# A tanh recurrence on 128 columns: one step as one block of 128 columns, or as two batches of 64 one behind the other

## The chip, the core and the metric

The kernel runs on one core of one Trainium2 chip. The metric is the device time of one execution in microseconds. The core has five engines that run side by side and meet through semaphores: TensorE (PE in the profile, with its weight loads shown apart as PEld), VectorE (DVE), ScalarE (ACT), GpSimd (POOL) and SyncE (SP, which issues most of the transfers here).

## The reference

An input `x` of 2 batches, 1024 positions and 256 features goes through a small recurrent network, and its states go through a mixture of experts whose result is added to `x`. What matters here is the recurrence:

```python
xW = jnp.einsum('ntd,dh->nth', x, Wx) + b
def step(prev_h, xw_t):
    next_h = jnp.tanh(xw_t + prev_h @ Wh)
    return (next_h, next_h)
_, hs = jax.lax.scan(step, h0, jnp.swapaxes(xW, 0, 1))
```

It runs over all 1024 positions of each of the 2 batches, with a state of 256 features. After it come 8 experts, of which each position takes the 2 with the largest logits:

```python
hidden = jax.nn.silu(x_flat @ wge.T) * (x_flat @ wue.T)
acc + we[:, None] * (hidden @ wde.T)
```

and the sum over the experts is added to the input `x`.

## The kernel before

**The recurrence in parallel.** The 1024 positions of a batch are cut into 64 pieces of 16 (`L = 16`), and all 64 pieces of both batches are stepped at once: the state is 256 features by 128 columns, where a column is a batch b and a piece q. A piece doesn't know the state at its start, so every piece starts early and runs over the pieces before it: these are the warm-up steps. Steps `s` from 8 to 47 warm up, and steps 48 to 63 give the states that are kept, in `hall`. A later check compares the states at the borders of the pieces; if one differs by more than a tolerance, a plain sequential version is run in place of the result.

**One step.** The 256 features are two halves of 128 partitions: `k` counts the halves of the old state, `j` those of the new. A step is, in this order:

- the seed, made two steps ahead: VectorE copies the input's share `xw` into two banks of PSUM, `acc[s % 2][0]` and `acc[s % 2][1]` (function `seed`), one bank for each half j, each 128 columns wide as (b, q). The copy is shifted by `sh` pieces, 3 to 0, so that a warm-up step reads the input of the piece before;
- four matmuls that add to these banks, `Wh` block (k, j) times the old state's half k, 128 columns each (line 611). The order of the four blocks alternates: on even steps (j, k) = (0,0), (1,0), (0,1), (1,1), on odd ones (0,0), (0,1), (1,0), (1,1). After two of them `run(s - 0.5)` emits what is planned for that moment;
- two tanhs on ScalarE (line 639), one for each half j, from the bank to the new state. They go through a helper that records line 49, as all VectorE, ScalarE and GpSimd instructions of this part do.

Up to step 27 (`S16 = 28`) state and weights are f16 in the matmuls; from step 28 on they are f32. From step 28 to step 47 the new state is a tile of shape [128, k, b, q] from a pool with three buffers, except at steps 31 and 47, where it is a tile `inj` that has the start state `h0` in one piece; q0 is then the first piece that the tanh writes. From step 48 on the state goes to `hall`.

**What runs beside it.** Other work is put into the recurrence by an order written out by hand: `at(step, ...)` notes it, `run(step)` emits it. For steps 28 to 47 these are the transfers of the first experts' weights (SyncE), the copy of the input to the output (SyncE, at 28), constant thresholds (GpSimd, at 40), and eight times, at steps 29, 31, 33 and 35 and at 37, 39, 41 and 43, a cast of 128x512 on ScalarE with a subtraction on VectorE behind it, which split the first expert's weights into a high and a low part. All instructions of one engine keep the program's order. After step 48 the routing (logits, one-hot tables, gathers) is worked in, and then follow the experts, which take most of the time.

Of the kernel before, what the change touches and what calls it, by code (L numbers as in the profile page):

```python
# [13 lines left out]
AF = mybir.ActivationFunctionType  # L14
# [5 lines left out]
P = 128  # L20
# [13 lines left out]
S16 = 28  # L34
# [18 lines left out]
def rnn_moe(ctx, tc, xT, xrows, h0T, Wx, Wh, b, gw, W, out):  # L53
    nc = tc.nc
    pe = tc.keep_in_program_order
    vec, act, pool = (InOrder(tc, e) for e in (nc.vector, nc.scalar, nc.gpsimd))
# [67 lines left out]
    def pgu_tile():  # L124
        return pgu.tile([P, 512], F32, name="pgu_t", tag="pgu")

    def ptr_tile():
        return ptp.tile([P, 512], F32, name="ptr", tag="ptr")
# [103 lines left out]
    def start_output():  # L232
# [9 lines left out]
    xw = [  # L242
        hidp.tile([P, 512], F32R, name=nm, tag=nm).bitcast(F32).rearrange("p (j i t) -> p j i t", j=2, i=2)
        for nm in ("hh", "hl")
        for _ in range(4)
    ]
    acc = [[pgu_tile()[:, 0:P] for j in range(2)] for a in range(2)]
# [3 lines left out]
    def fl(t):  # L251
        return t.rearrange("p b q -> p (b q)")

    def bq(t):
        return t.rearrange("p (b q) -> p b q", b=2)
# [17 lines left out]
    def x_split(n, k, eng, low=pool):  # L273
        m = order[n]
        hi, lo = (t[:, k, :] for t in xparts[n % 2])
        x = xs[k][:, m * 2 * P : (m + 1) * 2 * P]
        (act.copy if eng is act else eng.tensor_copy)(hi, x)
        low.tensor_tensor(lo, x, hi.bitcast(F32), ALU.subtract)

    def x_product(n, j):  # L280
        m = order[n]
        pt = ptr_tile()[:, 0 : 2 * P]
        ops = [(wxs[a][:, k, j * P : (j + 1) * P], xparts[n % 2][c][:, k, :]) for k in range(2) for a, c in ((0, 0), (1, 0), (0, 1))]
        for i, (l, r) in enumerate(ops):
            pe(nc.tensor.matmul(pt, lhsT=l, rhs=r, start=(i == 0), stop=(i == len(ops) - 1)))  # L285
        return pt

    def x_store(n, j, pt):
        vec.tensor_scalar(xw[order[n]][:, j].rearrange("p i t -> p (i t)"), pt, bs[:, j : j + 1], None, ALU.add)

    def seed(s, fresh=None):

        sh = 3 - s // L
        r = s % L
        for j in range(2):
            to = bq(acc[s % 2][j])[:, :, sh:64]
            if j == 1 and fresh is not None:
                vec.tensor_scalar(to, bq(fresh[:, r % 2 * P : (r % 2 + 1) * P])[:, :, 0 : 64 - sh], bs[:, j : j + 1], None, ALU.add)
            else:
                copy = act.copy if j == 1 and s >= 50 else vec.tensor_copy  # L300
                copy(to, bq(xw[r // 2][:, j, r % 2, :])[:, :, 0 : 64 - sh])
# [226 lines left out]
    def run(step):  # L528
        for t in sorted(t for t in todo if t <= step):
            for f in todo.pop(t):  # L530
                f()
# [53 lines left out]
    for s, q in ((15, 2), (31, 1), (47, 0)):  # L585
        t = rp.tile([P, 2, 2, 64], F16 if s + 1 < S16 else F32, name=f"inj{s}")
# [12 lines left out]
    vec.tensor_copy(wh16, wh)  # L599
    x_first(1)  # L600
    seed(S0 + 1)
    x_store(1, 0, x_product(1, 0))
    prev = None
    for s in range(S0, 64):
        if s > S0:
            blocks = [(0, 0), (1, 0), (0, 1), (1, 1)] if s % 2 == 0 else [(0, 0), (0, 1), (1, 0), (1, 1)]
            w = wh16 if s < S16 else wh
            for i, (j, k) in enumerate(blocks):
                if i == 2:
                    run(s - 0.5)  # L610
                pe(nc.tensor.matmul(acc[s % 2][j], lhsT=w[:, k, j * P : (j + 1) * P], rhs=prev[k], start=False, stop=True, skip_group_check=True))  # L611
        n, late = (s - S0 + 3) // 2, None
        if n < R // 2:
            pt = x_product(n, (s - S0 + 3) % 2)
            if s % 2 == 0:
                late = n, 1, pt
            else:
                x_store(n, 0, pt)
        elif s < S16:
            pt = ptr_tile()[:, 0:P]  # L620
            for _ in range(2):
                pe(nc.tensor.matmul(pt, lhsT=zl, rhs=zl, start=True, stop=True))  # L622
        q0 = 0
        if s in inj:
            t, q = inj[s]
            q0 = q + 1
            dst = [t[:, k] for k in range(2)]
        elif s >= 48:
            dst = [bq(hall[k][:, s - 48, :]) for k in range(2)]
        else:  # L630
            half = s + 1 < S16
            t = hp.tile([P, 2, 2, 64], F16 if half else F32, name="h16" if half else "h32")
            dst = [t[:, k] for k in range(2)]
        if s == S0:
            q0 = 3 - s // L
            pool.memset(t[:, :, :, 0:q0], 0.0)
        for j in range(2):
            x = bq(xw[s // 2][:, j, s % 2, :])[:, :, 0 : 64 - q0] if s == S0 else bq(acc[s % 2][j])[:, :, q0:64]
            act.activation(dst[j][:, :, q0:64], x, AF.Tanh)
        prev = [fl(d) for d in dst]  # L640
        if s + 2 < 64:
            seed(s + 2, late and late[2])
        if late:
            x_store(*late)
        if s == S0:
            for k in range(2):
                x_split(2, k, act)
        n = (s - S0 + 6) // 2
        if n < R // 2:
            x_split(n, (s - S0) % 2, act)  # L650
        run(s)
# [50 lines left out]
    with ExitStack() as c2:  # L702
# [207 lines left out]
        for n in range(len(steps)):  # L910
            i, s = steps[n]
            u = units[i]
            j = jobs.index(u.job)
# [25 lines left out]
            if 2 <= n < len(steps) - 2:  # L939
                v, t = done[n - 2]  # L940
# [4 lines left out]
        s = NIC - 4  # L945
# [175 lines left out]
```

## Time and profile before

| | us |
|---|---|
| Median of 3 runs (392.15 to 394.67) | 392.47 |
| The profiled execution, its own time | 396.46 |
| Its span, first to last instruction | 394.7 |
| TensorE busy in the span | 372.6 |
| TensorE weight loads busy | 349.5 |
| VectorE busy | 232.3 |
| ScalarE busy | 200.1 |
| GpSimd busy | 118.9 |

One execution was profiled, and every duration is from it. Engines overlap, so busy times don't add up to the span. A line of a group reads: source line, engine, operation, output and inputs with shapes, the number of instructions, then busy time and mean nanoseconds of one, then the idle time ahead of them and what ended it. A line of the timeline reads: start, duration, engine, source line, operation, shapes and count of merged instructions, and in brackets the idle time ahead of it with the engine that ended it. An f32 matmul of the source shows as two instructions on PE and two weight loads on PEld.

### The profile page before, as it was taken

The page shows a single profiled execution, that of the slowest core. Times are in us where ns is not written, and L with a number is a line of the kernel's source. Part 1 is how long each engine was busy: PE and PEld are TensorE (multiplying, and loading weights), DVE is VectorE, ACT ScalarE, POOL GpSimd, SP SyncE. Part 2 cuts the span into 40 slices and gives each one's busy share as a digit, 9 for nine tenths or more (in the row PEclk, how much of TensorE's full clock was granted, in tenths as well). Part 3 has the DMA queues.
Part 4 walks back from the last instruction along what each step waited for, and adds up shares of the span by engine and source line. Part 5 has one row for each costly group of instructions (what it writes and reads, how often), then busy time and mean ns, then how long its engine had stood idle before and what let it go on. Part 6 is the DMA issues. An engine that isn't in the chain of part 4 may idle for free.

```text
span 394.7 us, 7319 instructions
## 1 busy us (share of the span) xinstructions
PE 372.6 (94%) x2715; PEld 349.5 (89%) x2715; DVE 232.3 (59%) x619; ACT 200.1 (51%) x461; POOL 118.9 (30%) x124
## 2 busy tenths in 40 slices
PE   8999999989999999998999999999999999999980
PEld 7998798779997789998999999999989999999970
DVE  6867648897675665565636644465545656644220
ACT  4656676543654543656445553564455555435230
POOL 4770001204272401773042612432040024007032
PEclk9999999999999999999999999999999999999996
DMA  7962323542373433585234444345323306004013
GB/s 222 425 252 76 110 99 104 139 112 56 125 200 108 95 117 125 117 233 143 52 95 48 149 120 134 39 134 135 109 27 111 106 7 151 2 0 48 4 19 39
DMA packets 19291, 43.31 MB, mean 110 GB/s; under 512 B 4832, under 2 KB 14208, under 8 KB 16096
## 3 DMA queue, kind: packets, MB, share of 16 engines
q1 hardware_dynamic: 12432, 32.86, 24.9%
q0 software_dynamic: 6496, 9.09, 13.1%
q10 hardware_dynamic: 320, 0.80, 0.7%
q8 instruction: 24, 0.39, 0.4%
q14 instruction: 19, 0.16, 0.1%
HBM read 36.23 MB, written 10.22 MB: 118 GB/s over the span
## 4 chain that ended last, share of the span: by engine, by line
PE 76%; DMA 8%; DVE 6%; ACT 3%; issue 3%; POOL 1%; POOLq 0%; DVEq 0%; ACTq 0%
PE pgu_t L712 40%; PE yb L865 21%; PE pgu_t L611 8%; DMA out_dram<-y,si 8%; DVE wd L49 3%; PE ptr L285 3%; PE ptr L192 2%; PE pgu_t L865 1%; PE ptr L622 1%; ACT y L874 1%; ACT h L49 1%; PE ptr L339 1%; DMA xg<-rows_d,gidx 1%; DVE mi L49 1%; DVE pgu_t L49 1%
## 5 line engine op out<-in xcount | busy, mean ns | idle before, releaser
L865 PE MATMUL yb<-wd,hh 128*128 128x256 f32 (+2 forms) x560 | 97.7, 284 | 2.5 <-ACT y L874 2.5
L865 PEld LDWEIGHTS yb<-wd,hh 128*128 128x128 f32 (+2 forms) x560 | 83.0, 185 | 5.4 <-ACT y L874 3.7
L728 ACT CAST hh<-g 128x256 fp32r<-128x256 f32 (+5 forms) x96 | 46.7, 489 | 77.0 <-DVE g L720 70.4
L720 DVE TENSOR_TENSOR g<-g,pgu_t 128x256 f32<-128x256 f32 (+5 forms) x96 | 49.8, 522 | 57.0 <-PE pgu_t L712 40.3
L712 PE MATMUL pgu_t<-xhi,gu_g 128*128 128x256 f32 (+5 forms) x384 | 78.5, 326 | 1.3 <-ACT xhi L49 0.6
L453 POOL DMA_INDIRECT out_dram<-y,si x27 | 45.1, 1672 | 113.4 <-ACT y L874 108.8
L712 PE MATMUL pgu_t<-xhi,gu_u 128*128 128x256 f32 (+5 forms) x384 | 77.8, 324 | 0.0
L719 ACT ACTIVATE g<-pgu_t 128x256 f32<-128x256 f32 (+5 forms) x96 | 44.7, 466 | 55.2 <-PE pgu_t L712 50.8
L712 PEld LDWEIGHTS pgu_t<-xhi,gu_u 128*128 128x128 f32 x384 | 61.3, 188 | 4.3
L712 PEld LDWEIGHTS pgu_t<-xhi,gu_g 128*128 128x128 f32 x384 | 58.6, 189 | 4.3 <-issue 1.3
L729 DVE TENSOR_TENSOR hl<-g,hh 128x480 fp32r<-128x480 f32 (+4 forms) x56 | 33.6, 600 | 32.2 <-ACT hh L728 31.6
L865 PE MATMUL yb<-wd,hl 128*128 128x256 f32 (+1 forms) x184 | 51.8, 282 | 0.0
L446 POOL DMA_INDIRECT xg<-rows_d,gi x27 | 29.2, 1080 | 63.9 <-DVE cm L794 56.9
L712 PE MATMUL pgu_t<-xlo,gu_g 128*128 128x256 f32 (+5 forms) x192 | 47.0, 325 | 0.2 <-issue 0.2
L712 PE MATMUL pgu_t<-xlo,gu_u 128*128 128x256 f32 (+5 forms) x192 | 46.5, 323 | 0.0
L712 PEld LDWEIGHTS pgu_t<-xlo,gu_g 128*128 128x128 f32 x192 | 32.5, 188 | 3.0 <-DVE hh L729 0.6
L712 PEld LDWEIGHTS pgu_t<-xlo,gu_u 128*128 128x128 f32 x192 | 32.5, 188 | 2.2
L865 PEld LDWEIGHTS yb<-wd,hl 128*128 128x128 f32 (+1 forms) x184 | 33.7, 183 | 0.1
L611 PE MATMUL pgu_t<-h,wh 128*128 128x128 f32 (+1 forms) x224 | 28.6, 266 | 1.4
L729 DVE TENSOR_TENSOR hh<-g,hh 128x256 fp32r<-128x256 f32 x40 | 16.8, 424 | 14.2 <-ACT hh L728 11.5
L49 ACT ACTIVATE h<-pgu_t 128x128 f32<-128x128 f32 (+1 forms) x72 | 17.6, 276 | 13.9 <-PE pgu_t L611 8.7
L611 PEld LDWEIGHTS pgu_t<-h,wh 128*128 128x128 f32 x152 | 18.4, 190 | 4.2 <-ACT h L49 3.3
(162 smaller groups left out, 462.4 us busy)
## 6 DMA issues: line engine op xcount, KB each, us to landing
raw<-in_W_dram SPq DMA_DIRECT2D x24, 1024.0 KB, 5.0
gu_u<-in_xT_dram SPq DMA_DIRECT2D x6, 256.0 KB, 7.0
rows_e<-gu_u SPq DMA_DIRECT2D x4, 256.0 KB
rows_d<-rows_e SPq DMA_DIRECT2D x1, 528.0 KB
rows_d<-rows_e ACTq DMA_DIRECT2D x1, 528.0 KB, 4.3
out_dram<-in_xrows_dram SPq DMA_DIRECT2D x1, 512.0 KB
rows_d<-rows SPq DMA_DIRECT2D x2, 256.0 KB
rows_d<-gu_u SPq DMA_DIRECT2D x2, 256.0 KB
```

The source lines that it names most:

```text
L49: return lambda *a, **k: self.tc.keep_in_program_order(f(*a, **k))
L192: pe(nc.tensor.transpose(pt[:, m, j, :], tiles[i][:, k * (P + E) : k * (P + E) + P], ident))
L285: pe(nc.tensor.matmul(pt, lhsT=l, rhs=r, start=(i == 0), stop=(i == len(ops) - 1)))
L446: nc.gpsimd.indirect_dma_start(out=xg, out_offset=None, in_=rows[:, :], in_offset=bass.IndirectOffsetOnAxis(ap=idx, axis=0),)
L453: return nc.gpsimd.indirect_dma_start(out=out[:, :], out_offset=bass.IndirectOffsetOnAxis(ap=idx, axis=0), in_=y, in_offset=None, compute_ ...
L611: pe(nc.tensor.matmul(acc[s % 2][j], lhsT=w[:, k, j * P : (j + 1) * P], rhs=prev[k], start=False, stop=True, skip_group_check=True))
L712: pe(nc.tensor.matmul(pt, lhsT=a[i], rhs=b[j], start=(first and i + j + n == 0), stop=(j == 1 and n == len(lhs_rhs) - 1), skip_group_check ...
L719: nc.scalar.activation(g, pg, AF.Silu)
L720: nc.vector.tensor_tensor(g, g, pu, ALU.mult)
L728: nc.scalar.copy(hh, src)
L729: nc.vector.tensor_tensor(hl, src, hh.bitcast(F32), ALU.subtract)
L865: pe(nc.tensor.matmul(yt[0:w, :], lhsT=h[a][:, i * P : i * P + w], rhs=wd[b][:, ic, :], start=(ic == 0 and first and n == 0), stop=(ic == ...
```

## The change

In steps 28 to 47 the division of a step changes from halves to batches. The two banks now belong to the batches: bank z holds both halves j of batch z, 64 columns each, as (j, q). The seed is one copy for each batch. The matmuls are eight, of 64 columns: for batch 0 the four blocks with k outside and j inside, then `run(s - 0.5)`, then the same four blocks for batch 1. The tanhs are one for each batch, reading both halves from the bank and writing both halves of that batch into the state tile, whose layout stays. Steps before 28 and from 48 on are untouched.

```diff
@@ seed @@
         sh = 3 - s // L
         r = s % L
+        if S16 <= s < 48:
+            for z in range(2):
+                vec.tensor_copy(bq(acc[s % 2][z])[:, :, sh:64], xw[r // 2][:, :, r % 2, z * 64 : z * 64 + 64 - sh])
+            return
         for j in range(2):
             to = bq(acc[s % 2][j])[:, :, sh:64]
@@ the loop over s @@
             w = wh16 if s < S16 else wh
+            if S16 <= s < 48:
+
+                for z in range(2):
+                    if z == 1:
+                        run(s - 0.5)
+                    for k in range(2):
+                        for j in range(2):
+                            pe(nc.tensor.matmul(bq(acc[s % 2][z])[:, j, :], lhsT=w[:, k, j * P : (j + 1) * P], rhs=prev[k][:, z * 64 : z * 64 + 64], start=False, stop=True, skip_group_check=True))
+                blocks = ()
             for i, (j, k) in enumerate(blocks):
                 if i == 2:
                     run(s - 0.5)
...
         for j in range(2):
+            if S16 <= s < 48:
+                act.activation(t[:, :, j, q0:64], bq(acc[s % 2][j])[:, :, q0:64], AF.Tanh)
+                continue
             x = bq(xw[s // 2][:, j, s % 2, :])[:, :, 0 : 64 - q0] if s == S0 else bq(acc[s % 2][j])[:, :, q0:64]
             act.activation(dst[j][:, :, q0:64], x, AF.Tanh)
```

In the tanh's new line the loop's `j` counts batches: `t[:, :, j, q0:64]` is both halves of batch j.

## Prediction

> **What bounds the kernel now.** I read the page first (busy times, then the chain that ended last), then the chain in order of time over the recurrence, then the timeline of single steps, then the groups of TensorE kept apart by shape.
>
> ```profile
> PE 372.6 (94%) x2715; PEld 349.5 (89%) x2715; DVE 232.3 (59%) x619; ACT 200.1 (51%) x461; POOL 118.9 (30%) x124
> PE pgu_t L712 40%; PE yb L865 21%; PE pgu_t L611 8%; DMA out_dram<-y,si 8%; DVE wd L49 3%; PE ptr L285 3%; PE ptr L192 2%; PE pgu_t L865 1%; PE ptr L622 1%; ACT y L874 1%; ACT h L49 1%; PE ptr L339 1%; DMA xg<-rows_d,gidx 1%; DVE mi L49 1%; DVE pgu_t L49 1%
> ```
>
> The reader is to see that TensorE sets the time, and that the recurrence's products (L611) are on the ending chain. The change touches steps 28 to 47 alone. They begin with the first f32 run of L611, at 26.73, and end where step 48, the first to read the state `inj` written by step 47, loads its weights at 50.53:
>
> ```profile
> 26.73 0.97 PEld L611 LDWEIGHTS pgu_t<-h,wh 128*128 128x128 f32 x8
> ...
> 49.45 0.97 PEld L611 LDWEIGHTS pgu_t<-h,wh 128*128 128x128 f32 x8 [0.33 <-ACT h L49]
> 49.45 1.16 PE L611 MATMUL pgu_t<-h,wh 128*128 128x128 f32 x8
> 50.20 0.28 ACT L49 ACTIVATE inj<-pgu_t 128x126 f32<-128x126 f32 x1 [0.58 <-PE pgu_t L611]
> 50.51 0.29 DVE L49 COPY pgu_t<-hh 128x128 f32<-128x128 f32 x1 [0.56 <-ACT inj L49]
> 50.53 0.97 PEld L611 LDWEIGHTS pgu_t<-inj,wh 128*128 128x128 f32 x8
> 50.65 0.28 ACT L49 ACTIVATE inj<-pgu_t 128x126 f32<-128x126 f32 x1 [0.17 <-PE pgu_t L611]
> ```
>
> That is 23.80 us for 20 steps, 1.19 each. The x8 says that one f32 step, written as 4 matmuls, is 8 passes, each with a weight load of its own. Eight loads last 0.97 us and a single one 0.19 (below), so one begins every (0.97 - 0.19) / 7 = 0.111 us; 8 passes cost 0.89. The other 0.30 of a step is latency. The chain shows it:
>
> ```profile
> 47.08 2.03 PE pgu_t L611 x14
> 49.10 0.02 issue
> 49.13 0.28 ACT h L49
> 49.41 0.04 issue
> 49.45 2.03 PE pgu_t L611 x14
> ```
>
> Two steps take 2.38 us, in which TensorE issues 16 passes (1.78) and stands still for a tanh for the rest, 0.6. So the most that the change can win is 20 x 0.30 = 6 us, and only if the passes cost no more in total.
>
> What a pass of half the columns costs is decided by these rows (operation, stationary shape, mean ns):
>
> ```profile
> L611 PEld LDWEIGHTS pgu_t<-h,wh 128*128 128x128 f32 x152 | 18.4, 190 | 4.2 <-ACT h L49 3.3
> L865 PEld LDWEIGHTS yb<-wd,hh 128*96 128x96 f32 x48 | 6.7, 163 | 0.0
> L865 PEld LDWEIGHTS yb<-wd,hh 128*32 128x32 f32 x16 | 1.7, 109 | 0.1
> L425 PEld LDWEIGHTS <-wd 128*128 128x128 f16 x32 | 2.2, 97 | 0.9 <-DVE wd L49 0.3
> ```
>
> From 32 to 96 to 128 stationary columns an f32 load grows from 109 to 163 to 190 ns: 27 ns for each 32 columns, over a fixed 82. The part that can't overlap the next load is thus 4 x 27 = 108 ns at 128 columns, and 97 - 82 = 15 ns for f16. The 111 ns between f32 passes is therefore the price of the load, and about that of streaming 128 columns too; the two lie side by side.
>
> **What the Trainium skill says.** "TensorE: Matmul & The Clock Gate", section "LDWEIGHTS (loading the stationary operand)", gives a load as P / 1.2 ns with P the stationary columns: 107 ns for 128. The trace agrees (108 from the rows above), and nothing in it depends on the moving columns. The section "Weight-path perf modes" of the same page says that the fast weight load is on for inputs other than FP32; the trace agrees (15 ns against 108). The section "Back-to-back issue gap" says that the spacing in a stream of load and matmul pairs is set by both. "PSUM — Partial Sum Buffer", section "Summary: rules for kernel authors", wants reads during a matmul to go to another bank; before and after, each tanh reads a bank that is not being written.
>
> **The change part by part.**
>
> *Matmuls.* A step's 4 matmuls of 128 columns become 8 of 64: (k, j) for batch 0, then the same four blocks for batch 1. The weight block changes with every matmul, so none of the loads falls away: 16 passes and 16 loads a step in place of 8 and 8. Streaming 64 columns takes half of about 107 ns, so the load decides. I bound a pass from below by the load, 108, and from above by the largest spacing that passes with both a full f32 load and a comparable stream show here, 12 in 1.42 us at L712, 118 ns. I take 110: a little over the load, since a run of 8 today keeps to 111 while also streaming twice the columns. Step: 16 x 0.110 = 1.76 us.
>
> *The waits that go.* Within step 47 above, the first bank is complete with pass 4. Its load begins at 49.45 + 3 x 0.111 = 49.78, its matmul one load later at 49.90, and tanh begins at 50.20: 0.30 later, of which half a stream (0.05) falls away at 64 columns, 0.25 left. tanh lasts 0.28 (128 elements as before: both halves j of one batch), and 50.48 to 50.53 is 0.05 until the next load. With a step beginning at 0, batch 0's last matmul begins at 8 x 0.11 = 0.88, its tanh runs from 1.13 to 1.41, and batch 0 could go on at 1.46; TensorE is busy with batch 1 until 1.76. Cover: 0.30 us. For batch 1 it is the same, one half step on. All the 0.30 of latency a step is hidden; late next is TensorE itself.
>
> *ScalarE.* Two tanhs a step, as before. Eight times an f32 cast of 128x512 (0.61) stands between batch 1's tanh (ends 2.29) and the next tanh of batch 0 (ready at 2.89): it ends at 2.90. Delay 0.01 against 0.30 of cover: nothing. If the passes were faster, this cover would shrink (rival 2).
>
> *VectorE.* Two seed copies a step as before (0.29 each), of one batch with both halves in place of one half with both batches, 128x124 or 128x126 elements either way. They wait for that batch's tanh of step s and are needed at step s + 2, over 1.5 us later even behind a 0.69 us subtraction. Nothing.
>
> *SyncE, POOL.* The work planned between the blocks by `run(s - 0.5)` is empty for steps 28 to 47 (all its due times there are whole numbers), and no DMA moves in the order.
>
> *The two ends.* Step 28 starts as now: its k = 1 blocks are 4 passes behind its k = 0 blocks in either order. Step 48 has whole-width operands again and needs both tanhs of step 47, so the latency of batch 1's is exposed once: last matmul at 26.73 + 20 x 1.76 = 61.93, tanh 62.18 to 62.46, next load 62.51. From there on all is as before.
>
> *Sum.* Step 48 begins at 62.51 and not at 50.53: 11.98 us later (35.20 + 0.58 - 23.80). Does the rest give some of it back? In the stretch from 50.5 to 76.0, TensorE is busy 24.26 of 25.50 us, from 120 to 385 it is busy 260.32 of 265.00, and its waits between are for ACT, DVE and gathers that the routing itself starts; all of them move with the recurrence. The weights of the first experts land earlier than needed now and have still more time. I give back nothing. The profiled execution took 396.46 us (span 394.7, the rest around it); it would become 408.4. The median of the runs shown is 392.47, 4 us lower than the profiled one; the same addition gives 404.5, or 3.1% more.
>
> **The rivals.**
>
> 1. *False wait between the batches.* A tanh now writes a strided region (two halves, one batch), interleaved with the other batch's. If the k = 1 blocks of batch 0 were made to wait for batch 1's tanh too, they could start at 0.25 + 0.28 + 0.05 + 0.01 = 0.59 after the step's start and not at 0.44, plus a load of 0.11 to refill: 0.25 a step, 5 us, 409.5. Against it: POOL's write of the probabilities into `rows`, interleaved in the same way with two transfers out of that tile, carries no wait for those transfers in the trace's records. Chance 0.05.
>
> 2. *Passes go by moving columns (the other side).* If a pass of 64 columns took half, about 0.058, a step's 16 passes would be 0.93, and the loop of one batch would decide: 8 x 0.058 + 0.25 + 0.28 + 0.05 = 1.05. The eight casts would then push batch 0's tanh by about 0.3 each, 2.3 us. 20 x 1.05 + 2.3 + 0.5 = 23.8: no change, 392.5; without the casts' delay 390. For it: the f16 passes of L425 (8 in 0.61) come every 55 ns, at the stream's rate. Against it: their loads cost 15 ns and these 108. It decides as soon as a pass is under 1.19 / 16 = 0.074. Chance 0.06, of which half is a gain over 1%.
>
> 3. *Load and stream no longer overlap.* A pass would be 108 + 53 = 161 ns, a step 2.58, in all 28 us more: 420.7. For it, only that 64-column f32 passes are not in this trace; against it, load and stream of 128 columns overlap now (111, not 215). Chance 0.04.
>
> 4. *Part is absorbed later*, if the longer recurrence lets early transfers finish before the gathers: TensorE's waits for gathers are only 0.17 and 0.48, so at most some 1 to 4 us, 401. Chance 0.05.
>
> **How the numbers follow.** The forecast, slower with 110 ns a pass, has 0.80. With 108 ns it gives 34.56 + 0.58 - 23.80 = 11.3, so 403.8; with 118 ns 37.76 + 0.58 - 23.80 = 14.5, so 407.0. Widened by a part of rivals 1 and 4, the range is 402.3 to 408.3. Slower by over 1%, which is about what a measurement of this kernel can tell from no change, holds the forecast, rivals 1 and 3, and all of 4: 0.93 with a little rounding down for the unforeseen; within 1%: 0.04; faster by over 1%: 0.03.
>
> **What would show it.** In the changed profile L611 should have 160 more matmul passes and loads than now, f32 with 64 moving columns, beginning every 0.108 to 0.112 us without a gap through steps 28 to 47; no TensorE wait for ACT there; two ACT rows of 128 elements a step, about 0.9 us apart; step 48 beginning near 62.5; and a stretch after it of the same length as now. Spacing under 0.074 us, or ACT waits on TensorE with short passes, would make the forecast wrong, as would a later stage that is over 3 us shorter.

## The result, and the profile after

The changed kernel takes 406.46 us in the median of 4 runs (405.98 to 407.15), the kernel before 392.6 (the median of 4 runs, one more than in the table above): 1.0342 times as long, with an interval of 1.0313 to 1.0371. That is 13.9 us more. The profiled execution took 405.98 us, with a span of 404.1.

The page's first lines of the changed kernel:

```profile
span 404.1 us, 7658 instructions
PE 385.0 (95%) x2875; PEld 366.5 (91%) x2875; DVE 233.8 (58%) x619; ACT 201.0 (50%) x461; POOL 119.7 (30%) x124
```

TensorE has 160 more matmul passes and 160 more weight loads, as the change asks for; the counts of the other engines in this line have not moved. The page's chain of what ended last stops here at a single transfer and shows nothing of the recurrence, so the timeline has to carry the reading. It shows the first steps of the changed stretch:

```profile
27.38 5.77 PEld L619 LDWEIGHTS pgu_t<-h,wh 128*128 128x128 f32 x51
27.46 5.71 PE L619 MATMUL pgu_t<-h,wh 128*128 128x64 f32 x50
...
28.52 0.28 ACT L49 ACTIVATE h<-pgu_t 128x128 f32<-128x128 f32 x1 [1.03 <-PE pgu_t L619]
...
29.41 0.28 ACT L49 ACTIVATE h<-pgu_t 128x128 f32<-128x128 f32 x1 [0.62 <-PE pgu_t L619]
```

A tanh comes every 0.89 us, which is 8 passes, and it is ScalarE that waits for TensorE (1.03 us before the first tanh, then 0.62, in brackets). TensorE waits for no tanh: the loads of this stretch have no idle time before them. 51 loads in a row last 5.77 us: (5.77 - 0.19) / 50 = 0.1116 us from one to the next. The group of the passes of 64 columns shows this idle time in its last column:

```profile
L619 PEld LDWEIGHTS pgu_t<-h,wh 128*128 128x128 f32 x304 | 34.1, 192 | 0.0
L619 PE MATMUL pgu_t<-h,wh 128*128 128x64 f32 x304 | 34.2, 275 | 0.0
```

Where whole-width steps begin again (line 624, step 48), the one exposed wait is seen:

```profile
63.36 0.28 ACT L49 ACTIVATE inj<-pgu_t 128x126 f32<-128x126 f32 x1 [0.62 <-PE pgu_t L619]
...
63.69 0.63 PEld L624 LDWEIGHTS pgu_t<-inj,wh 128*128 128x128 f32 x5 [0.50 <-ACT inj L49]
```

Steps 28 to 47 thus last from 27.38 to 63.69, 36.31 us in place of 23.80: 12.5 us more. A pass of 64 columns costs what one of 128 cost, 0.112 us against 0.111.

### The profile page after: what moved, and what is told of

Read it like the earlier page. It is cut to its first block, busy times and chain, and to the rows that moved or that the text cites. A ratio compares the mean times of both kernels' runs of the same rounds, so it can differ in the third digit from the quotient of the medians.

```text
span 404.1 us, 7658 instructions
## 1 busy us (share of the span) xinstructions
PE 385.0 (95%) x2875; PEld 366.5 (91%) x2875; DVE 233.8 (58%) x619; ACT 201.0 (50%) x461; POOL 119.7 (30%) x124
## 3 DMA queue, kind: packets, MB, share of 16 engines
HBM read 36.23 MB, written 10.22 MB: 115 GB/s over the span
## 5 line engine op out<-in xcount | busy, mean ns | idle before, releaser
L619 PE MATMUL pgu_t<-h,wh 128*128 128x64 f32 x304 | 34.2, 275 | 0.0
L619 PEld LDWEIGHTS pgu_t<-h,wh 128*128 128x128 f32 x304 | 34.1, 192 | 0.0
L745 DVE TENSOR_TENSOR hh<-g,hh 128x256 fp32r<-128x256 f32 x40 | 16.9, 424 | 12.8 <-ACT hh L744 12.5
```

The lines of the kernel that those rows point to most:

```text
L619: pe(nc.tensor.matmul(bq(acc[s % 2][z])[:, j, :], lhsT=w[:, k, j * P : (j + 1) * P], rhs=prev[k][:, z * 64 : z * 64 + 64], start=False, st ...
L745: nc.vector.tensor_tensor(hl, src, hh.bitcast(F32), ALU.subtract)
```

## Experiments

**A second profile of the kernel before.** The first one had waits in the early experts that the changed kernel did not have, which makes a comparison of two single profiles doubtful.

> The kernel before once more, for a second profile. In the first one the span was 394.7 us and TensorE waited in the stretch from 118 to 131 us, at the start of the second expert, for about 1.1 us (xhi, a semaphore, ACT y), which the changed kernel's profile does not show. Theory (these waits belong to that one execution): a span near 391, with the recurrence's steps 28 to 47 again 23.8 us long, and the 3 us shorter stretch from 97 to 147 us. Rival (the change itself shortened the later stages): the waits are there again.

Its time was 393.37 us, its span 391.5. The first table below is this second profile by stage, the second one the changed kernel. A row begins with the stretch and its length; after the comma come busy us and number of instructions of PE, PEld, DVE, ACT and POOL, then the granted TensorE clock, the DMA share and GB/s. The stretches are steps 28 to 47; from step 48 to the first product of the first expert; from there to two groups of transposes among the experts (the third and the fourth row end there); and the rest, to the last matmul.

```profile
27.47:51.28 23.81, 22.37 (x163) 19.37 (x162) 15.47 (x49) 14.44 (x48) 1.05 (x10) 1.00 0.35 115
51.28:80.25 28.97, 26.33 (x243) 24.66 (x243) 22.07 (x142) 18.81 (x70) 3.85 (x8) 1.00 0.39 109
80.25:114.00 33.75, 32.33 (x290) 31.75 (x291) 27.22 (x95) 17.56 (x38) 14.43 (x14) 1.00 0.39 104
114.00:144.60 30.60, 30.60 (x179) 26.59 (x178) 19.88 (x31) 16.25 (x27) 9.67 (x8) 1.00 0.46 137
144.60:379.20 234.60, 233.60 (x1627) 223.26 (x1625) 127.79 (x231) 117.80 (x224) 67.56 (x46) 1.00 0.35 88
```

```profile
27.38:63.69 36.31, 35.94 (x324) 35.81 (x322) 16.71 (x50) 15.23 (x49) 1.06 (x10) 1.00 0.26 88
63.69:92.74 29.05, 26.21 (x243) 24.66 (x243) 21.77 (x141) 18.48 (x69) 3.85 (x8) 1.00 0.35 94
92.74:127.10 34.36, 32.56 (x291) 31.84 (x292) 27.11 (x95) 17.68 (x38) 14.34 (x14) 1.00 0.39 104
127.10:157.70 30.60, 30.60 (x179) 26.57 (x178) 19.87 (x31) 16.22 (x27) 9.63 (x8) 1.00 0.45 134
157.70:392.30 234.60, 233.60 (x1627) 223.26 (x1625) 127.77 (x231) 117.79 (x224) 67.56 (x46) 1.00 0.34 88
```

The recurrence's stretch grew by 12.50 us. The last two stretches are equally long, the two between differ by 0.1 and 0.6. In the first profile of before the last three stretches were 35.34, 32.50 and 235.50 long, so its waits belonged to that execution, and the change neither gave time to the later stages nor took any that these profiles can tell from such scatter. The other traces of the next sections bear this out. From the first load of step 48 to the start of the last matmul it is 327.9 us in the second profile of before, 328.5 and 328.3 in the changed kernel's two profiles, 328.4 with half of the steps changed and 328.4 with the matmuls cut alone; with f16 steps it is 328.3 without the change and 327.7 with it. Which kernels carry the change can't be read from these lengths.

**The changed kernel once more.**

> The changed kernel once more, beside the others on the same chip: 1.034 times the kernel before. Its profile should show the same 0.112 us between passes of 64 columns.

406.46 us against 392.82: 1.0334, interval 1.0309 to 1.0359. The span was again 404.1, and steps 28 to 47 again last 36.3 us, in which the 320 loads come every 0.112 us.

**Half of the steps.**

```diff
-if S16 <= s < 48:
+if S16 <= s < 38:
```

(at the change's three places)

> The change is made in steps 28 to 37 alone, half of the 20; steps 38 to 47 are as before. Theory (each changed step pays 8 more weight loads of 0.112 us and wins back about 0.30 us of waiting): half of the recurrence's loss, 10 x (1.787 - 1.19) + 0.4 at the border where whole-width steps begin again = 6.4 us, so near 399 us. Rival (the loss is a single cost at the end of the warm-up or in the later stages, whatever the number of steps): as large as with all 20 steps, 13 to 14 us, near 406. If 1.3 us of the 13.9 were such a single cost: 7.7, near 400.3.

399.68 us, 1.0169 times before (1.0144 to 1.0193), 6.86 us more: half the loss for half the steps, so the loss is paid step by step. Its profiled execution was the slowest of the six, 402.7 us; step 28 began there at 29.95, 2 to 3 us later than in the other profiles, so only the length of the stretch is read from it. Steps 28 to 47 are 30.3 us long, 6.5 more than before. Where whole-width steps begin again, now at step 38, the wait of the whole change comes again:

```profile
48.39 0.97 PEld L624 LDWEIGHTS pgu_t<-h,wh 128*128 128x128 f32 x8 [0.50 <-ACT h L49]
```

**Only the cut of the matmuls.** The banks, the blocks' order and the tanhs stay those of before. The edit is shown shortened; it holds for steps 28 to 47 alone.

```diff
-pe(nc.tensor.matmul(acc[s % 2][j], lhsT=..., rhs=prev[k], ...))
+for z in range(2):
+    zz = slice(z * 64, z * 64 + 64)
+    pe(nc.tensor.matmul(acc[s % 2][j][:, zz], lhsT=..., rhs=prev[k][:, zz], ...))
```

> Steps 28 to 47 keep the banks, the order of blocks and the tanhs of before (one for each half j); only each matmul of 128 columns is cut into two of 64. So the loads are paid and no batch runs ahead of the other. Theory (loads cost 0.112 each, the batches' independence wins the waits back): 16 passes a step are 1.79 us; tanh of the first half is complete 4 passes before an even step's end, so every second step still waits about 0.2 to 0.3: 20 x 1.787 + 10 x 0.25 = 38.2 for the 20 steps against 23.8 before, 14.5 us more than before, near 407, and about 2 us slower than the changed kernel. Rival (the bank and tanh division costs time too): faster than the changed kernel.

406.77 us, 1.0353 (1.0329 to 1.0376), not separable from the changed kernel by its time. The traces part them: from the first f32 matmul of step 28 to the first of step 48, this kernel takes 37.02 us, the changed one 36.23, the kernel before 23.72.

```profile
27.77:64.79 37.02, 37.02 (x322) 36.45 (x321) 17.34 (x49) 14.89 (x48) 0.97 (x10) 1.00 0.26 87
27.46:63.69 36.23, 35.86 (x323) 35.73 (x321) 16.63 (x50) 15.15 (x49) 0.98 (x10) 1.00 0.26 88
27.56:51.28 23.72, 22.28 (x162) 19.28 (x161) 15.38 (x49) 14.35 (x48) 0.96 (x10) 1.00 0.35 115
```

(cut alone; the whole change; before.) The direction was right, the size not: 0.8 us and not 2. Merely having 16 passes in a step leaves less of tanh uncovered than I reckoned: (37.02 - 20 x 1.787) / 10 = 0.13 us for every two steps and not 0.25. In the trace this is one wait for every two steps, behind the even step.

The size can be worked out, as an estimate from these traces. When the next step waits for a tanh on 64-column passes, its first pass comes about 0.58 us later than it would without the wait, if nothing else ran in between (0.57 at step 48 of the changed kernel). In the kernel cut alone, 4 passes still stand behind the last one of the first half in an even step and 8 in an odd one. They take 0.45 and 0.89 us, so 0.13 is left open in the one and nothing in the other. In the kernel before there were 2 and 4 passes for about 0.63 us (half a stream more), which leaves 0.41 and 0.19: the 0.6 us of two steps. Doubling the passes thus closes most of the gaps by itself, whichever batch the passes belong to. The independence of the two batches, for which the change divides banks and tanhs, removes the last ten waits of 0.13 us, but exposes one of 0.57 at step 48: 0.8 us net.

**What a pass costs.** Blocks of unused matmuls, all of this form:

```diff
+pt = ptr_tile()
+for i in range(24):
+    pe(nc.tensor.matmul(pt[:, 0:64], lhsT=wh[:, i % 2, i // 2 % 2 * P : i // 2 % 2 * P + 128], rhs=ident[:, 0:64], start=True, stop=True))
```

> The kernel before with eight blocks of 24 matmuls each put on TensorE behind the recurrence, whose results nothing reads. Stationary columns x moving columns: f32 128x128, 128x64, 128x16, 128x64 with one and the same stationary block, 64x64, 64x128, 32x16, and f16 128x64. Spacing of passes by theory (the weight load decides, 108 to 112 ns for 128 stationary columns, in proportion to them; the stream about 0.83 ns a moving column of an f32 pass): 112, 112, 112, 112, 56 to 60, 112, 28 to 35, f16 about 32. Rival A (a floor for every f32 pass, whatever its shape): 112 in all seven. Rival B (the moving columns decide): 112, 58, 25, 58, 58, 112, 25. Rival C (a repeated block is not loaded again): the fourth near 58 with the second at 112.

The timeline's loads of the blocks 128x128, 128x64, repeated 128x64, 64x128, 32x16 and f16 128x64 (start, length of the row, stationary shape, count):

```profile
77.50 5.44 PEld L655 LDWEIGHTS ptr<-ident,wh 128*128 128x128 f32 x48
82.86 5.44 PEld L658 LDWEIGHTS ptr<-ident,wh 128*128 128x128 f32 x48
95.72 10.36 PEld L664 LDWEIGHTS ptr<-ident,wh 128*128 128x128 f32 x48
109.92 5.22 PEld L670 LDWEIGHTS ptr<-ident,wh 128*64 128x64 f32 x48
115.31 1.59 PEld L673 LDWEIGHTS ptr<-ident,wh 128*32 128x32 f32 x48 [0.17 <-issue]
116.93 0.76 PEld L676 LDWEIGHTS <-wh 128*128 128x128 f16 x24
```

Taking a single load off each row and dividing by the steps between: with 128 stationary columns, 128 and 64 moving columns cost the same, (5.44 - 0.19) / 47 = 111.7 ns. With 32 x 16 it is (1.59 - 0.11) / 47 = 31.5 ns. With 64 stationary and 128 moving columns it is (5.22 - 0.14) / 47 = 108 ns, and there the stream decides. The f16 block goes at (0.76 - 0.10) / 23 = 29 ns. Rivals A and B fall. The blocks of 16 moving columns and of 64 x 64 are left out, because the granted clock changed inside them; before it did, the passes of 16 moving columns, too, came every 112 ns. The repeated stationary could not be read, because the granted clock fell in this stretch:

```profile
82.90:88.20 5.30, 5.30 (x51) 5.30 (x49) 0.00 (x0) 0.00 (x0) 0.00 (x0) 1.00 0.01 3
91.00:95.60 4.60, 4.60 (x25) 4.60 (x24) 0.00 (x0) 0.00 (x0) 0.00 (x0) 0.52 0.00 0
95.60:106.00 10.40, 10.40 (x50) 10.40 (x50) 0.00 (x0) 0.00 (x0) 0.00 (x0) 0.50 0.00 0
```

(The third number from the end is the clock; the second row lies in the block of 16 moving columns.)

> Again unused blocks of 24 f32 matmuls behind the recurrence of the kernel before, in an order that keeps the array busier, because in the first such kernel the granted clock fell to a half within the block of 16 moving columns and stayed there through the block with one repeated stationary. Stationary x moving columns: 128x64 repeated stationary, 128x128, 64x64, 128x128, 96x64, 128x128, 128x32. Theory (a pass is 0.83 ns for each stationary column and 5 ns more): 112, 112, 58, 112, 85, 112, 112. Rival (a repeated stationary is not loaded again): the first near 58.

In this order the clock held until the last block. Repeated stationary 128x64, 64x64 and 96x64:

```profile
77.52 5.44 PEld L655 LDWEIGHTS ptr<-ident,wh 128*128 128x128 f32 x48
88.44 2.87 PEld L661 LDWEIGHTS ptr<-ident,wh 128*64 128x64 f32 x48
96.74 4.18 PEld L667 LDWEIGHTS ptr<-ident,wh 128*96 128x96 f32 x48
```

They give 111.7, (2.87 - 0.14) / 47 = 58 and (4.18 - 0.16) / 47 = 85.5 ns. A stationary block that repeats is loaded again at full price, so rival C falls too. From 32, 64, 96 and 128 stationary columns (31.5, 58, 85.5, 111.7) an f32 pass costs 0.835 ns a stationary column and about 5 ns more, as long as its stream is shorter than that. (The 64 x 64 pass is near that border: half of the 108 ns that 128 moving columns take would be 54.)

**The change without dear loads.** Both kernels keep the f16 form of the recurrence to step 47.

```diff
-S16 = 28
+S16 = 48
-TOL = 2.0**-18
+TOL = 1.0
```

In the second kernel, which has the change, its three conditions then read `28 <= s < 48`.

> The kernel before with the f16 form of the recurrence kept up to step 47 in place of 27 (with the two filler matmuls that these steps have) and the tolerance of the border check raised to 1. Its numbers are coarser; it is the base for the next kernel. An f16 step takes 0.72 to 0.75 us now and an f32 one 1.19: 20 x 0.45 = 9 us less than before, near 383.5.

386.1 us, 0.9822 (0.9796 to 0.9848). The expected 9 us less came out as 6.4: a step takes 0.80 and not 0.72 to 0.75, from 31.17 to 43.93 for steps 32 to 47:

```profile
31.17 0.43 PE L611 MATMUL pgu_t<-inj,wh 128*128 128x128 f16 x4
...
43.93 0.85 PE L611 MATMUL pgu_t<-inj,wh 128*128 128x128 f32 x6
```

> The same with the change made in steps 28 to 47 on f16 operands: 8 matmuls of 64 columns and a tanh for each batch. A step has 8 single passes in place of 4, each with a load that is cheap (15 ns). Theory (the price of the change is the f32 weight load): no such price here, so within 2 us of the f16 kernel without the change, near 383.5. Rival (more matmuls, semaphores or the new division of banks cost time by themselves): slower than that kernel by 5 us or more.

384.13 us, 0.9789 (0.9768 to 0.981); steps 32 to 47 last from 30.07 to 42.48, 0.776 each:

```profile
30.07 0.43 PE L619 MATMUL pgu_t<-inj,wh 128*128 128x64 f16 x8
...
42.48 0.94 PE L624 MATMUL pgu_t<-inj,wh 128*128 128x128 f32 x6
```

So the same division, with the same four additional matmuls a step and the same new use of banks and tanhs, costs nothing measurable where the loads are cheap. It even takes 0.35 us off these 16 steps; the rest of the 2 us between the medians lies outside these steps, and the two intervals overlap. What remains of a step is seen in its chain, the two filler matmuls of an f16 step (L635, four f32 passes) and the 8 passes (L619) in turn, with no wait between:

```profile
30.50 0.53 PE ptr L635 x4
31.02 0.23 PE pgu_t L619 x8
```

TensorE is thus nearly filled here: by the prices above, 4 x 0.112 + 8 x 0.029 = 0.68 of the 0.776 us (an estimate). A cost of up to 0.1 us a step could hide in the rest, but not the 0.6 us that a divided f32 step costs.

No run points to a version that beats the kernel before at its own precision: as these kernels write their matmuls, an f32 step divided by columns pays its 8 loads twice.

## Why the prediction was right

The forecast was 404.5 us with a range of 402.3 to 408.3; measured were 406.46. Its mechanism is shown by the runs, step by step.

- *16 loads and passes a step, priced by the load.* Shown by the blocks of matmuls and, with the loads made cheap, by the f16 pair. The price was put at 0.110 and is 0.1117. The prediction had 0.111 from its own row of 8 loads and went below it, because half the stream was to make a pass a little cheaper; it did not. Over 320 passes this is 0.5 us, the one term of the sum that was mis-sized. That 128 moving columns stream in about 107 ns was only argued; the block of 64 stationary columns gives 108. The 15 ns for an f16 load were a difference of two kinds of load; the f16 block shows only that load and stream together take 29 ns.
- *All waits between steps covered.* Right: batch 0's first tanh was to begin 1.13 us after the step and begins at 28.52 - 27.38 = 1.14; the loads have no idle time. But the reason was only partly right. The prediction put it down to batches that run independently; the kernel cut alone has no such batches and is still rid of all but 1.3 of the 6 us of waiting, since the additional passes themselves fill the time.
- *ScalarE's casts and VectorE's copies cost nothing.* In the changed kernel's trace the cast of step 29 ends at 31.98, and the next tanh begins when it is due, at 32.09. The loads, which would show a late tanh, have no idle time.
- *The end at step 48.* 0.58 was reckoned beyond the passes; 36.31 - 20 x 1.787 = 0.57 was measured.
- *Nothing given back later.* Right within the scatter of the traces, 327.7 to 328.5 us from step 48 on with the change or without it; only the first profile of before (332.1) lies outside, by its waits in the early experts.

For the recurrence 11.98 us more were predicted and 12.50 measured; the rest of the 2 us between 404.5 and 406.46 is in the medians. The medians differ by 13.9 in the first comparison and 13.6 in the second; 12.5 us lies in both intervals (12.3 to 14.6 and 12.1 to 14.1 when multiplied out). The last 1 us has no place in the traces. The profiled executions of the two kernels, 405.98 and 393.37 us, lie 12.6 apart, and 11 executions of the kernel before spread from 392.1 to 394.5. So scatter is likely, but it isn't shown.

Rival 1 (a false wait between the batches) would have shown idle time, and rival 3 (load and stream one behind the other) 161 ns a pass; there is neither. Rival 2 (passes by moving columns) is refuted by 111.7 ns at both 64 and 128. Rival 4 (absorbed later) would have needed a shorter stretch after step 48.

## What to carry to other kernels

Before a matmul is cut along its moving columns, price a pass as the longer of its weight load and its stream: here, in f32 with 128 stationary columns, the two were in balance at 128 moving columns (111.7 and 108 ns), so cutting them in two doubled the cost. Independent chains only help an engine that is waiting, and the wait to be won (0.30 us a step here) must be larger than the work that makes the chains independent (8 x 0.112). The same cut was free with f16 operands, where a pass of 64 columns takes 29 ns, so the verdict belongs to the data type and not to the idea. And before a gap is put down to dependence, count how many passes stand between a result and its use: here more passes alone closed most of the gaps.

## What was not expected of the hardware

The granted clock fell to a half while TensorE issued f32 passes back to back, when these had few moving columns: about 26 passes into the block of 16 moving columns (from 111.7 to 213 ns a pass), and about 36 passes into the block of 32 in the second such kernel. With 64 moving columns it stayed at 1.00 through the 36 us of the changed kernel. But once it was down, the same shape did not bring it back: the block with one repeated stationary, 64 moving columns as well, ran its whole 10.4 us at 0.50, with TensorE busy in all of it, and the clock rose again only within the next block, 64 x 64. A busy row on TensorE is thus enough neither to keep its clock nor to raise it. What the exact condition is, these runs don't show; each of the two kernels was executed once.
